# Two copies and a sum of the first layer moved off VectorE: last states to ScalarE, the sum over directions to identity products

## The chip, the cores and the metric

The kernel runs on one core of one Trainium2 chip. The metric is the device time of one execution in microseconds (us): the median of three runs of the kernel before is 18365.06 us, between 18352.45 and 18369.7. A core has five engines with a queue each: TensorE (PE in the profile; its weight loads are PEld), VectorE (DVE), ScalarE (ACT), GpSimd (POOL) and SyncE (SP, which issues DMAs). Each works through its instructions in a fixed order and waits at an instruction until what it needs is there; what stands behind that instruction waits too.

## What is computed

The network has two layers; the change concerns only the mixing part of the first. There, eight images of 64x64 pixels with 128 channels pass through a state-space scan in four directions (rows forward and backward, columns forward and backward), and the four results are weighted and added:

```python
U = jnp.stack([xp, jnp.flip(xp, 1), x_tb, jnp.flip(x_tb, 1)], 0)
Y = jax.vmap(_mamba)(U, ...)
# in _mamba, for each of 128 channels and 16 states:
#   h = exp(dt * A) * h + (dt * x) * B ;  y = sum over states of h * C
#   y = (y + x * D) * silu(z) ;  return y @ out_w.T
y_fused = gate[0] * y_lr + gate[1] * y_rl + gate[2] * y_tb + gate[3] * y_bt
```

The gate, the output weights and the final projection are folded into one 128x128 matrix for each direction, so the kernel only has to add four products into one image-sized result.

## The kernel before

**Tiles.** A direction `d` of an image (4096 pixels) is cut into four chunks `j` of `CH` = 1024 pixels; a chunk has 16 groups of 8 channels with their 16 states, 128 rows in all. A group of a chunk is one slot `n` of the loop in `scan_blocks` (line 703): 8 images x 4 directions x 4 chunks x 16 groups = 2048 slots. Below, slot 0 to 15 count within a chunk.

**One slot.** In slot `n`, TensorE spreads the decays of group `n+1` to its 128 rows by six bf16 products into a PSUM tile `dA` (128x1024, two banks, two such tiles), and ScalarE takes their exponential in place. GpSimd multiplies `bx` for group `n+2`. VectorE then runs the scan of group `n` in place in its `dA` (line 765), multiplies it by `C` into `hc` (line 335), and copies the last column of the scan to `last[:, q]` (a 128x1 copy, line 347), from which the same group of the next chunk starts its scan. The last chunk of a direction (`j` = 3) makes no such copy. A `dA` tile is free for group `n+2` when VectorE has read it.

**A chunk's end.** The output of a chunk gathers in one PSUM tile `y` (two banks), and is finished in the first slots of the next chunk. In slot 1, VectorE multiplies `y` by the gate `zs` (`gate_y`). At the start of slot 2, ahead of the products for the decays of group 3, TensorE multiplies `zs` by the output matrix, half by half, back into `y` (`out_product`; at 17.5 in the table, and halves are rounded up and put at the start of the slot). Then `out_add` brings the two halves of 512 pixels to `r`, the image in SBUF: for `d` = 0 ScalarE copies them, for the other directions VectorE adds them to what stands in `r`. For directions 1 and 3 the result is reversed on the way; for directions 2 and 3 it is also transposed, so that `r` is read and written with 64 elements between neighbours.

**The next chunk.** In slots 1 to 4, ScalarE and VectorE also compute the step sizes of the chunk that starts at the next slot 0, for two halves (0 and 1): ScalarE `relu_abs`, `exp`, `plus_one` (`sp_u`), then VectorE `lost` (line 344, which reads `sp_u`), ScalarE `ln`, and VectorE `dt` (two operations on 512 columns). `plus_one(0)` and the second `relu_abs` stand in slot 2, `exp(1)`, `plus_one(1)`, `lost(0)`, `lost(1)`, `ln(0)` and `dt(0)` in slot 3, `ln(1)` and `dt(1)` in slot 4.

**The next image.** While an image is scanned, `input_steps` normalises the next one in eight pieces, one in each chunk. Of a piece's steps, `powers` (two ScalarE activations) falls in slot 2, `second_log` and `unskipped` (two more) in slot 4, of the eight chunks that follow chunks 5 to 12 of an image's sixteen (counted from 0). These stand ahead of the chunk's own steps on the queue.

**Order.** `ordered` (used by `mm`, `act`, `tt`, `copy` and others) chains every recorded instruction behind the one before it on its engine, so the order on each engine is that of the loop: in a slot first the steps at half slots, then the decays and exponential of group `n+1`, `bx`, the scan, `hc` and `last`, and then the table's steps of the slot.

Of the kernel before, what the change touches and what calls it, by code (L numbers as in the profile page):

```python
# [12 lines left out]
ALU = mybir.AluOpType  # L13
# [9 lines left out]
L = 4096  # L23
S = 512
# [5 lines left out]
CH = 1024  # L30
# [239 lines left out]
def bc(ap, n, axis=None):  # L270

    axis = len(ap.shape) if axis is None else axis
    v = ap.unsqueeze(axis)
    shape = list(v.shape)
    shape[axis] = n
    return v.to_broadcast(shape)


class Net:
# [167 lines left out]
    def scan_steps(self, ch, xp, r, pl, ps):  # L447
# [4 lines left out]
        nc, d, j = self.nc, ch["d"], ch["j"]  # L452
        pool = nc.gpsimd
        back = d % 2 == 1
        lo = L - CH * (j + 1) if back else CH * j
        dtb, cb2 = self.w(f"dt_b{d}"), self.cb2[:, d : d + 1]
        start = [lo + (1 - q if back else q) * S for q in range(2)]
        half = [slice(q * S, (q + 1) * S) for q in range(2)]
        ID, TANH = AF.Identity, AF.Tanh
        v = {}  # L460

        def order(ap):
            return ap[:, ::-1] if back else ap
# [5 lines left out]
        def make(name, bufs, width=S):  # L469
            t = v[name] = pl.tile([C, width], F32, name=name.rstrip("01"), bufs=bufs)  # L470
            return t
# [4 lines left out]
                o = start[q] + (6 - t if back else t)  # L476
                self.mm(p, self.Wt[:, d, t, :], xp[:, o : o + S], start=t == 0, stop=t == 3)

        def gate(name, to, q, **kw):
            p = v[f"{name}{q}"]  # L480
            self.act(order(to[:, half[q]]), p, ID, scale=0.5, **kw)
            th = make(f"th{q}", 2)
            self.act(order(th), p, TANH, scale=0.5, **kw)
            self.act(th, th, ID, bias=self.k("one"))

        def gated(of, name, q):
            to = of[name][:, half[q]]
            self.tt(to, to, v[f"th{q}"], ALU.mult, pool)

        def x_gate(q):  # L490
            if q == 0:
                ch["xs"] = make("xs", 3, CH)
            gate("x", ch["xs"], q, bias=cb2)

        def z_product(q):
            self.mm(bank(f"z{q}"), self.w(f"z_w{d}"), xp[:, start[q] + PAD : start[q] + PAD + S])
# [1 line left out]
        def z_gate(q):  # L498
            if q == 0:
                make("zs", 1, CH)  # L500
            gate("z", v["zs"], q)

        def dt_product(q):
            self.mm(bank(f"d{q}"), self.Wd[:, d, :], ch["xs"][:, half[q]])
# [58 lines left out]
                self.mm(ch["y"][rows_, half[q]], self.D_diag[:, rows_], ch["xs"][:, half[q]], start=False)  # L563

        def gate_y():
            self.tt(v["zs"], ch["y"], v["zs"], ALU.mult)

        def out_product(q):
            self.mm(ch["y"][:, half[q]], self.Wo[:, d, :], v["zs"][:, half[q]])

        def out_add(q):
            p, lo = ch["y"][:, half[q]], CH * j + q * S
            lo = L - S - lo if back else lo
            if d < 2:
                to = r[:, lo : lo + S]
                to = to[:, ::-1] if back else to
            else:
                w0 = lo // 64
                to = r.rearrange("p (h w) -> p w h", w=64)[:, w0 : w0 + S // 64, :]
                to = to[:, ::-1, ::-1] if back else to  # L580
                p = p.rearrange("p (w h) -> p w h", h=64)
            if d == 0:
                self.ordered(nc.scalar.copy(to, p))
            else:
                self.tt(to, to, p, ALU.add)

        table = [
            (-23, taps, 0, (0, 1)), (-22, taps, 0, (2, 3)), (-21, taps, 1, (0,)), (-20, taps, 1, (1,)),
            (-19, taps, 1, (2, 3)), (-21, x_gate, 0), (-18, x_gate, 1), (-20, gated, ch, "xs", 0), (-17, gated, ch, "xs", 1),
            (-16, dt_product, 0), (-15, dt_product, 1), (-16, self.table, EXP_LN_SET),  # L590
            (-15, relu_abs, 0), (-15, exp, 0), (-14, plus_one, 0), (-14, relu_abs, 1), (-13, exp, 1), (-13, plus_one, 1),
# [4 lines left out]
            (-9, self.table, EXP_TANH_SET), (-8, part, 1, 1), (-8, rest, 1, 0), (-7, rest, 1, 1),  # L596
            *([(12, diagonal)] if j == 0 else []),
            (7, z_product, 0), (8, z_product, 1), (8, z_gate, 0), (9, z_gate, 1),
            (10, gated, v, "zs", 0), (11, gated, v, "zs", 1),
            (16, skip, 0), (16, skip, 1), (17, gate_y), (17.5, out_product, 0), (17.5, out_product, 1),  # L600
            (18, out_add, 0), (18, out_add, 1),
        ]
        return table
# [99 lines left out]
    def scan_blocks(self, r, xp, xt, pl, ps):  # L703
# [4 lines left out]
        nc = self.nc  # L708
# [27 lines left out]
        last = None  # L736
        for n in range(min(todo), max(todo) + 1):
            for step, args in ahead.pop(n, ()):
                step(*args)
            u = n + 1  # L740
            if 0 <= u < total:

                ch, q = chunks[u // NQ], 4 * (u % 4) + u % NQ // 4
                dA[u] = ps.tile([128, CH], F32, tag="dA", bufs=2, name="dA")
                sel = self.expand[:, 8 * q : 8 * q + 8, :].rearrange("p c n -> p (c n)")
                for h in range(2):
                    sg = slice(h * S, (h + 1) * S)
                    for i in range(3):
                        self.mm(dA[u][:, sg], sel, ch["parts"][:, i, sg], start=i == 0, stop=i == 2)
                self.act(dA[u], dA[u], AF.Exp, scale=self.negA[:, ch["d"] * NQ + q : ch["d"] * NQ + q + 1])  # L750
            u = n + 2
            if 0 <= u < total:
                bx[u] = pl.tile([128, CH], F32, name="bx", bufs=4)
                self.tt(bx[u], xE.pop(u), chunks[u // NQ]["B16"], ALU.mult, nc.gpsimd)
            u = n + 4
            if 0 <= u < total:
                ch, q = chunks[u // NQ], 4 * (u % 4) + u % NQ // 4
                xE[u] = pl.tile([128, CH], F32, name="xE", bufs=4)
                nc.sync.dma_start(xE[u], bc(ch["dtx"][8 * q : 8 * q + 8, :], NST, 1))
            if 0 <= n < total:  # L760
                ch, q = chunks[n // NQ], 4 * (n % 4) + n % NQ // 4
                if n % NQ == 0 and ch["j"] == 0:
                    last = pl.tile([128, NQ], F32, name="last", bufs=2)
                t = dA.pop(n)
                self.ordered(nc.vector.tensor_tensor_scan(  # L765
                    out=t, data0=t, data1=bx.pop(n), initial=0.0 if ch["j"] == 0 else last[:, q : q + 1],
                    op0=ALU.mult, op1=ALU.add,
                ))
                hcs[n] = pl.tile([128, CH], F32, name="hc", bufs=5)
                self.tt(hcs[n], t, ch["C16"], ALU.mult)  # L770
                if ch["j"] < NCH - 1:
                    self.copy(last[:, q : q + 1], t[:, CH - 1 :], nc.vector)
            if n % 4 == 0 and 4 <= n < total + 4:
                g0 = n - 4
                ch, k = chunks[g0 // NQ], g0 % NQ // 4
                if k == 0:
                    ch["y"] = ps.tile([C, CH], F32, tag="y", bufs=1, name="y")
                for h in range(2):
                    for g in range(4):
                        self.mm(ch["y"][32 * g : 32 * g + 32, h * S : (h + 1) * S],  # L780
                                self.k("collect")[:, 32 * k : 32 * k + 32],
                                hcs[g0 + g][:, h * S : (h + 1) * S], start=k == 0, stop=False)
                for g in range(4):
                    del hcs[g0 + g]
            for step, args in todo.pop(n, ()):
                step(*args)
# [1116 lines left out]
```

## Time and profile before

| what | value |
| --- | --- |
| median of 3 runs | 18365.06 us |
| the profiled execution | 18370.72 us, its span 18368.8 us |
| end of the first layer's scans | the last add to `r` starts at 8525.3 us |
| VectorE busy from 2000 to 4000 us | 1931 of 2000 us |
| TensorE, GpSimd, ScalarE busy there | 1581, 1600, 1214 us |
| scan, 1536 that start from `last` | 2350 ns each |
| `hc` | 1225 ns each |
| copy to `last`, 1536 | 148 ns each |
| add to `r`, 192 | 675 ns least, 1259 ns median |
| copy to `r` by ScalarE (`d` = 0), 64 | 592 ns each |

The profile is one execution recorded by the hardware. A row of a timeline gives the start in us, the duration in us, the engine, the line (often that of a helper), the operation, the tiles written and read, and the count; in square brackets stands how long the engine had been idle before, and what released it. Where an instruction is a matrix product of fp32, TensorE shows two records for one `matmul`.

### The profile page before, as it was taken

The numbers are of one execution on the slowest core, as the hardware profiler recorded it, in microseconds if no ns is written. First come the engines' busy times: TensorE is split into PE (matmuls) and PEld (weight loads), VectorE is DVE, ScalarE is ACT, GpSimd is POOL, SyncE is SP. The second block draws the span as 40 slices with busy tenths as digits, with TensorE's granted clock in tenths as the row PEclk, the third lists the DMA queues.
The fourth block names the chain that finished last, engine by engine and source line by source line (L and its number), as shares of the span: only waits on it lengthen the run. The fifth ranks groups of instructions, "written<-read, shape, count | busy, mean of one in ns | idle before, by whom it ended". The sixth has DMA issues, their size and how long they took to land. (4 is left out here: it accounts for less than half of the span.)

```text
span 18368.8 us, 300240 instructions
## 1 busy us (share of the span) xinstructions
PE 15729.2 (86%) x114341; PEld 8435.2 (46%) x114341; DVE 15174.0 (83%) x20453; ACT 11208.4 (61%) x15902; POOL 9306.3 (51%) x6308
## 2 busy tenths in 40 slices
PE   7777777787777778776887999999999999998998
PEld 2222222222222222223644677777777777774443
DVE  7999999999999999998264677777777777777886
ACT  5656666565666656554253667776777767676553
POOL 7878788787878878774011222222222222222444
PEclk9999999999999999998698999999999999998999
DMA  4555555555455555553442111111111111111222
GB/s 131 143 144 147 145 145 143 143 144 146 143 144 146 142 146 145 143 138 112 140 146 68 28 31 30 30 31 31 31 29 31 31 31 29 31 31 40 93 95 82
DMA packets 843742, 1734.86 MB, mean 94 GB/s; under 512 B 184315, under 2 KB 416667, under 8 KB 833883
## 3 DMA queue, kind: packets, MB, share of 16 engines
q1 hardware_dynamic: 842302, 1715.66, 32.6%
q8 instruction: 904, 14.81, 0.3%
q14 instruction: 536, 4.39, 0.1%
HBM read 1474.28 MB, written 241.04 MB: 93 GB/s over the span
## 5 line engine op out<-in xcount | busy, mean ns | idle before, releaser
L335 POOL TENSOR_TENSOR bx<-xE,B 128x1024 f32<-128x1024 f32 x2048 | 4811.6, 2359 | 320.8 <-DMA xE<-dtx_d 161.8
L288 PE MATMUL dA<-parts,expand 128*128 128x512 bf16 x12288 | 3194.6, 399 | 1719.2 <-DVE last L347 1301.2
L296 ACT ACTIVATE dA<-dA,negA 128x1024 f32<-128x1024 f32 x2048 | 2229.8, 1089 | 2948.9 <-PE dA L288 2942.4
L765 DVE TENSOR_TENSOR_SCAN dA<-dA,last,bx 128x1024 f32<-128x1024 f32 x1536 | 3609.7, 2350 | 91.1 <-ACT dA L296 81.3
L288 PEld LDWEIGHTS <-expand 128*128 128x128 bf16 x12288 | 1128.1, 100 | 4140.1 <-DVE last L347 2110.4
L344 DVE SCALAR_TENSOR_TENSOR E_cm<-E_cm,gm_cm 128x1024 f32<-128x1024 f32 x2048 | 2440.5, 1227 | 280.2 <-ACT E_cm L296 267.6
L335 DVE TENSOR_TENSOR hc<-dA,C 128x1024 f32<-128x1024 f32 x2048 | 2508.2, 1225 | 107.8 <-DVE dA L765 1.8
L1279 POOL COPY Sd_cm<-S_cm 64x128 f32<-64x128 f32 x1024 | 882.7, 862 | 2622.5 <-DVE S_cm L335 2533.1
L296 ACT ACTIVATE E_cm<-ss_p 128x1024 f32<-128x1024 f32 x2048 | 1981.5, 1021 | 266.0 <-PE ss_p L288 253.1
L335 POOL TENSOR_TENSOR xD_cm<-tok_cm,D_cm 128x256 f32<-128x256 f32 x512 | 404.5, 790 | 2374.0 <-PE y_p L288 2306.8
L288 PE MATMUL y_p<-E_cm,pad_cm 128*32 128x128 f32 x32768 | 1321.3, 277 | 119.6 <-DVE E_cm L344 118.6
L765 DVE TENSOR_TENSOR_SCAN dA<-dA,bx 128x1024 f32<-128x1024 f32 x512 | 1172.3, 2290 | 50.5 <-ACT dA L296 42.9
L288 PE MATMUL ss_p<-ssB_cm,ssA_cm 128*128 128x512 bf16 x4096 | 1090.5, 383 | 71.9 <-DVE gm_cm L335 44.2
L288 PE MATMUL y<-hc,kt 128*32 128x512 f32 x8192 | 1087.7, 651 | 3.6 <-DVE hc L335 3.6
L288 PEld LDWEIGHTS y_p<-E_cm,pad_cm 128*32 128x32 f32 x32768 | 903.7, 110 | 369.1 <-DVE E_cm L344 202.5
L288 PE MATMUL bc_p<-stk_cm,W_cm 128*128 128x256 f32 x4096 | 943.2, 384 | 26.4 <-DMA stk_cm<-xs 20.8
L1136 DVE COPY dtr_cm<-tok_p 128x16 f32<-128x16 f32 x1024 | 176.8, 173 | 867.1 <-ACT tok_cm L296 867.1
L288 PEld LDWEIGHTS bc_p<-stk_cm,W_cm 128*128 128x128 f32 x4096 | 770.8, 191 | 167.3 <-issue 28.4
L288 PE MATMUL tok_p<-W_cm,stk_cm 128*128 128x200 f32 x4096 | 749.5, 336 | 0.0
L344 DVE SCALAR_TENSOR_TENSOR dw<-h,w_second,dw 128x512 f32<-128x512 f32 x1024 | 723.1, 748 | 1.5 <-ACT h L296 1.1
L296 ACT ACTIVATE tok_cm<-tok_p 128x384 f32<-128x384 f32 x1024 | 503.1, 491 | 345.5 <-DVE dtr_cm L1136 183.0
L288 PEld LDWEIGHTS tok_p<-W_cm,stk_cm 128*128 128x128 f32 x4096 | 683.1, 190 | 52.2 <-ACT BC_cm L296 48.5
(432 smaller groups left out, 29590.8 us busy)
## 6 DMA issues: line engine op xcount, KB each, us to landing
xE<-dtx_d SPq DMA_DIRECT2D x2048, 512.0 KB
dtx_d<-dtx SPq DMA_DIRECT2D x256, 256.0 KB
x<-x SPq DMA_DIRECT2D x256, 256.0 KB
pb<-p_d SPq DMA_DIRECT2D x64, 1024.0 KB
ssA_cm<-cs_cm SPq DMA_DIRECT2D x3072, 4.0 KB
stk_cm<-xs SPq DMA_DIRECT2D x368, 128.0 KB
stk_cm<-y SPq DMA_DIRECT2D x368, 128.0 KB
px<-r SPq DMA_DIRECT2D x64, 256.0 KB
```

The costliest lines, as they stand in the source:

```text
L288: return self.ordered(self.nc.tensor.matmul(out, lhsT=lhsT, rhs=rhs, start=start, stop=stop))
L296: i = self.ordered(self.nc.scalar.activation(out, in_, func, **kw))
L335: self.ordered((eng or self.nc.vector).tensor_tensor(out, a, b, op))
L344: self.ordered(self.nc.vector.scalar_tensor_tensor(out=out, in0=a, scalar=s, in1=b, op0=op0, op1=op1))
L765: self.ordered(nc.vector.tensor_tensor_scan(out=t, data0=t, data1=bx.pop(n), initial=0.0 if ch["j"] == 0 else last[:, q : q + 1], op0=ALU. ...
L1136: nc.vector.tensor_copy(dtr[:, c, jj, :], v[:, :, cfg.wsil :])
L1279: nc.gpsimd.tensor_copy(Sd[gr, :, g * hi : (g + 1) * hi], S2[gr])
```

## The change

The 1536 copies to `last` become ScalarE copies, at the same place of the loop, which on ScalarE is behind the exponential of group `n+1`. For directions 1 to 3, each half of the output is followed by a product of the identity matrix with the piece of `r` that it is to be added to, accumulated in the same PSUM bank, and ScalarE copies the sum back to `r`, as it did for `d` = 0. So that the sum needs no reversal, `zs` of the backward directions is now written in the image's order, and `gate_y` reads `y` reversed.

```diff
-        def gate(name, to, q, **kw):
+        def gate(name, to, q, order=order, **kw):
             p = v[f"{name}{q}"]
-            self.act(order(to[:, half[q]]), p, ID, scale=0.5, **kw)
+            self.act(order(to), p, ID, scale=0.5, **kw)
...
-            to = of[name][:, half[q]]
+            to = of[name][:, half[1 - q if back and name == "zs" else q]]
...
-            gate("x", ch["xs"], q, bias=cb2)
+            gate("x", ch["xs"][:, half[q]], q, bias=cb2)
...
-            gate("z", v["zs"], q)
+            gate("z", v["zs"][:, half[1 - q if back else q]], q, lambda ap: ap)
...
         def gate_y():
-            self.tt(v["zs"], ch["y"], v["zs"], ALU.mult)
+            self.tt(v["zs"], order(ch["y"]), v["zs"], ALU.mult)
+
+        def rows_of(ap, q):
+            at = lo + q * S
+            if d < 2:
+                return ap[:, at : at + S]
+            return ap.rearrange("p (h w) -> p w h", w=64)[:, at // 64 : (at + S) // 64, :]
+
+        def out_bank(q):
+            p = ch["y"][:, half[q]]
+            return p if d < 2 else p.rearrange("p (w h) -> p w h", h=64)
 
         def out_product(q):
-            self.mm(ch["y"][:, half[q]], self.Wo[:, d, :], v["zs"][:, half[q]])
+            self.mm(ch["y"][:, half[q]], self.Wo[:, d, :], v["zs"][:, half[q]], stop=d == 0)
+            if d:
+                self.mm(out_bank(q), self.k("ident"), rows_of(r, q), start=False)
 
         def out_add(q):
...
-            if d == 0:
-                self.ordered(nc.scalar.copy(to, p))
-            else:
-                self.tt(to, to, p, ALU.add)
+            self.ordered(nc.scalar.copy(rows_of(r, q), out_bank(q)))
...
                 if ch["j"] < NCH - 1:
-                    self.copy(last[:, q : q + 1], t[:, CH - 1 :], nc.vector)
+                    self.ordered(nc.scalar.copy(last[:, q : q + 1], t[:, CH - 1 :]))
```

More of the change, by code (lines that the diff above doesn't have):

```diff
@@ L565, in gate_y @@
         def gate_y():
-            self.tt(v["zs"], ch["y"], v["zs"], ALU.mult)
+            self.tt(v["zs"], order(ch["y"]), v["zs"], ALU.mult)
[7 more added lines that the diff above has]
+            return p if d < 2 else p.rearrange("p (w h) -> p w h", h=64)
         def out_product(q):
-            self.mm(ch["y"][:, half[q]], self.Wo[:, d, :], v["zs"][:, half[q]])
+            self.mm(ch["y"][:, half[q]], self.Wo[:, d, :], v["zs"][:, half[q]], stop=d == 0)
+            if d:
+                self.mm(out_bank(q), self.k("ident"), rows_of(r, q), start=False)
         def out_add(q):
[L572 to L576, printed above, removed]
-            else:
[L578 to L581, printed above, removed]
-            if d == 0:
-                self.ordered(nc.scalar.copy(to, p))
-            else:
-                self.tt(to, to, p, ALU.add)
+            self.ordered(nc.scalar.copy(rows_of(r, q), out_bank(q)))
         table = [
```

## The prediction

> **What bounds the kernel now.** I read first the busy times, for the whole span and for a stretch of the first layer, then VectorE's groups there, then its timeline in undisturbed slots, and last the engines' timelines where a chunk is finished. The first layer's scans end at about 8.5 ms; the rest of the 18.4 ms is not touched.
>
> ```profile
> span 18368.8 us, 300240 instructions
> ...
> core 0: us, PE busy (x) PEld busy (x) DVE busy (x) ACT busy (x) POOL busy (x), PEclk, DMA share, GB/s
> 2000.00:4000.00 2000.00, 1580.91 (x6551) 552.01 (x6552) 1930.98 (x1611) 1213.88 (x1616) 1599.96 (x879) 0.95 0.52 144
> ```
>
> VectorE is busy 97% of the stretch: it is the bound, and whatever it waits for is added to the span. ScalarE has 61%, which looks like room, but an average says nothing of the slots where a chunk is finished.
>
> ```profile
> L347 DVE COPY last<-dA 128x1 f32<-128x1 f32 x1277 | 188.6, 148 | 0.0
> L335 DVE TENSOR_TENSOR r<-r,y x192: 675/1259/1293, 457.9 to 8525.3; 128x512 f32<-128x512 f32 x192
> L583 ACT COPY r<-y x64: 588/592/597, 198.6 to 7742.5; 128x512 f32<-128x512 f32 x64
> ```
>
> The first row is a group's busy time and mean; the other two give shortest/median/longest. An add to `r` takes 675 ns for direction 1 (reversed) and about 1260 ns for 2 and 3 (transposed).
>
> ```profile
> 3722.24 2.36 DVE L765 TENSOR_TENSOR_SCAN dA<-dA,last,bx 128x1024 f32<-128x1024 f32 x1
> 3724.63 1.22 DVE L335 TENSOR_TENSOR hc<-dA,C 128x1024 f32<-128x1024 f32 x1
> 3725.77 0.15 DVE L347 COPY last<-dA 128x1 f32<-128x1 f32 x1
> 3725.84 2.35 DVE L765 TENSOR_TENSOR_SCAN dA<-dA,last,bx 128x1024 f32<-128x1024 f32 x1
> 3728.22 1.22 DVE L335 TENSOR_TENSOR hc<-dA,C 128x1024 f32<-128x1024 f32 x1
> 3729.36 2.35 DVE L765 TENSOR_TENSOR_SCAN dA<-dA,last,bx 128x1024 f32<-128x1024 f32 x1
> ```
>
> Here a chunk with copies passes into one without (`j` = 3). The slot with the copy lasts 3.60 us (3.59 is usual), that without 3.52: a copy is worth 0.067 us, not its 148 ns, since it overlaps its neighbours.
>
> Now the finish of a chunk of direction 0, where ScalarE already copies and VectorE adds nothing (slots 2 and 3):
>
> ```profile
> 3409.17 1.98 PE L288 MATMUL y<-zs,W_out 128*128 128x512 f32 x4 [0.66 <-DVE zs L335]
> 3410.99 1.46 PE L288 MATMUL dA<-parts,expand 128*128 128x512 bf16 x6
> 3412.49 1.09 ACT L296 ACTIVATE dA<-dA,negA 128x1024 f32<-128x1024 f32 x1 [1.94 <-PE dA L288]
> 3413.50 1.07 ACT L583 COPY r<-y 128x512 f32<-128x512 f32 x2
> 3413.68 2.36 DVE L765 TENSOR_TENSOR_SCAN dA<-dA,last,bx 128x1024 f32<-128x1024 f32 x1 [0.97 <-ACT dA L296]
> ...
> 3418.53 0.70 DVE L344 SCALAR_TENSOR_TENSOR m<-sp_u,m 128x512 f32<-128x512 f32 x1 [0.57 <-ACT sp_u L296]
> ...
> 3420.47 2.35 DVE L765 TENSOR_TENSOR_SCAN dA<-dA,last,bx 128x1024 f32<-128x1024 f32 x1
> ```
>
> and of direction 2, where VectorE adds:
>
> ```profile
> 3931.32 1.98 PE L288 MATMUL y<-zs,W_out 128*128 128x512 f32 x4
> 3933.14 1.46 PE L288 MATMUL dA<-parts,expand 128*128 128x512 bf16 x6
> ...
> 3935.16 2.45 DVE L335 TENSOR_TENSOR r<-r,y 128x512 f32<-128x512 f32 x2
> ...
> 3937.50 2.35 DVE L765 TENSOR_TENSOR_SCAN dA<-dA,last,bx 128x1024 f32<-128x1024 f32 x1
> ...
> 3943.82 2.35 DVE L765 TENSOR_TENSOR_SCAN dA<-dA,last,bx 128x1024 f32<-128x1024 f32 x1
> ```
>
> In direction 0 the time without adds is not won: scan 3 waits 0.97 us for its exponential, which stands behind the output products on TensorE, and `lost(1)` waits 0.57 us for ScalarE, which made the copies first. In direction 2 the adds fill exactly this hole. From scan 2 to scan 4 (scan starts in VectorE's timeline, averaged over the six middle images) it takes 10.9 us after direction 0, 11.1 after 1, 12.2 after 2 and 3.
>
> **The change, part by part.** Removed copies to `last`: 12 of a chunk's 16 slots end on VectorE's own work (scans 2, 3 and 4 and slot 1 end on the waits above), so 12 x 0.067 = 0.8 us in each of 96 chunks: **-77 us**. The new ScalarE copy has no row of its shape; the nearest, an activation of 128x8 out of PSUM, takes 177 ns, so I take 0.2 us (ends 0.1 and 0.3). In a plain slot it is hidden: it stands behind the exponential for group n+1, which ends some 0.85 us before scan n+1 wants it (a plain one in the same trace ends at 3925.54, and its scan starts at 3926.39). Without that cover it would cost 0.2 us a slot. It is not hidden in slots 2 and 3, below.
>
> Sum over directions, TensorE. Two more fp32 products are four more records, which start 0.455 us apart in the rows above ((3933.14 - 3931.32) / 4): +1.82 us ahead of the products for decay 3, and nothing else stands there. Exponential 3 is late by as much; behind it on ScalarE wait the copy to `last`, the `powers`, the two copies to `r` and the step sizes; VectorE waits at scan 3 and then at `lost(1)`.
>
> The price of a boundary follows from direction 0. From the end of `gate_y` (about 3409.03) to scan 4 (3420.47) it takes 11.44 us. The new boundary is that plus 1.82 plus two small copies in the chain, 0.4: 13.66 us, and `powers` add 1.2 (the two activations take 0.66 + 0.53 us of ScalarE there). Before, from the same point, it is about 11.5 after direction 1 and 12.65 after 2 and 3 (the averages above and some 0.4 us of wait for exponential 2). So each boundary loses: direction 1 2.15, with `powers` 3.35; directions 2 and 3 1.0, with `powers` 2.2. That is with the adds' 1.2 and 2.4 us already taken off.
>
> `powers` are there after chunks 5 to 12: three of direction 1, four of 2, one of 3. An image: 2.15 + 3 x 3.35 + 4 x 2.2 + 2.2 + 3 x 1.0 = 26.2; the last image has none: 4 x 2.15 + 8 x 1.0 = 16.6. 7 x 26.2 + 16.6 = 200, less 24 chunks without copies to `last` x 0.4: **+190 us**. Direction 0 gets the two small copies alone, 24 x 0.4: **+10 us**.
>
> Slot 4. There the small copy waits for scan 4, which starts only after `dt(0)`; ScalarE used to be past that. Behind it stand `second_log` and `unskipped` (0.61 us each) and `ln(1)` (0.62), for which VectorE waits at `dt(1)`: ready 0.3 + 1.2 + 0.6 + 0.1 = 2.2 us after scan 4, when `hc` leaves VectorE free after 1.25. 0.9 us in 6 of the 8 such chunks of seven images, 42 x 0.9: **+38 us**. In slot 6 the copies of the input steps come 0.2 us later and hold a TensorE product that already waits for them: 42 x 0.2, **+8 us**. Where no input step is there, `ln(1)` is ready after 1.0 us and hidden by `hc`.
>
> The transposed `r` (directions 2 and 3, 64 boundaries). No row has TensorE read, or ScalarE write, with 64 elements between neighbours. The nearest is the same tile in VectorE's add: 1259 against 675 ns, 1.14 ns an element more, but there both sides are strided. [...] By the row's extra, the two copies cost 2 x 0.58 and the four records 4 x 0.58 = 2.3 us; by nothing, 0. [...] For ScalarE I take a doubling of the streamed part, 2 x 512 x 0.83 ns = 0.85 us (0.83 from 1021 ns for 1024 and 597 for 512 columns in its exponentials); for TensorE, where no row is near, about half of a doubling, 0.9. Both lie in the chain: 64 x 1.75 = **+112 us**, ends 0 and 64 x 3.5 = 225.
>
> `zs` written unreversed costs nothing (all 256 writes take 588 to 592 ns, reversed or not). `gate_y` reading reversed: the reversed add took 675 ns where a plain operation of that size takes 686, so nothing; at the doubling of the transposed row it would be 64 x 1.2 = 77.
>
> **Sum**: -77 + 190 + 10 + 38 + 8 + 112 = +281 us, on a span of 18368.8 within 18370.7; on the median of 18365, **18645 us**.
>
> **Rivals.** (1) Transposed access is free: 18645 - 112 = 18534. For it: no row of these engines shows a price. (2) It costs as much on each as on VectorE: 18645 + 113 = 18758. Both are ends of the same forecast. (3) VectorE stays the bound and what it loses in work is won: 64 boundaries x 2.35 + 32 x 1.2 + 77 = 266 us, **18100**. Its place is slot 2; it holds if output products, decay products and exponential 3 end before `hc` of group 2. They need 1.82 + 1.82 + 1.5 + 1.1 = 6.2 us after `gate_y` and have 3.6 to 3.9; it decides from 2.4 us less. VectorE's 97% speak for it, direction 0 against it. (4) The small copies hold up ScalarE in every slot, since each waits for the scan: 1536 x 0.2 on top, about 18950. Against it stands the 0.85 us of room. (5) The new waits are made good in later slots by what the removed work frees, and it ends level, 18365; but the plain slots before show VectorE without a wait that could shrink.
>
> **Numbers.** The forecast with its two ends 0.74 (own range 18534 to 18758), (3) 0.09, (4) 0.11, (5) 0.06. A change under 0.2% (37 us) can't be told from none: faster 0.09, same 0.05, slower 0.86. For 8 in 10 the range reaches a little beyond the ends: 18470 to 18790.
>
> **What would show it.** In the profile after: no VectorE row for `last` or `r`; VectorE idle before scan 3 for exponential 3 (2 to 4 us) and before `lost(1)` for `sp_u`, after directions 1 to 3; plain slots of 3.52 us; idle before `dt(1)` in chunks with input steps; TensorE's identity records and ScalarE's `r` copies longer for directions 2 and 3 if the strides cost. It is wrong if scan 3 starts on time, if plain slots are not shorter, or if the small copies take much over 0.3 us.

## The result

The changed kernel takes 18820.63 us (median of 4 runs, 18809.22 to 18830.5) where the kernel before takes 18360.6: a ratio of 1.0249, 95% interval 1.0237 to 1.0262. It is 460 us slower. Forecast were 281 us more, 18645, in a range of 18470 to 18790: the direction was right, the size was not, and the time lies 31 us beyond the range. (18360.6 is a median of four runs; the 18365 that the forecast started from is one of three.)

### The profile page after: what moved, and what is told of

It is laid out like the page before. It is cut to its first block, busy times and chain, and to the rows that moved or that the text cites. A ratio compares the mean times of both kernels' runs of the same rounds, so it can differ in the third digit from the quotient of the medians.

```text
span 18807.4 us, 299313 instructions
## 1 busy us (share of the span) xinstructions
PE 15986.3 (85%) x113668; PEld 8605.5 (46%) x114725; DVE 14884.6 (79%) x18725; ACT 11483.7 (61%) x17630; POOL 9304.5 (49%) x6308
## 5 line engine op out<-in xcount | busy, mean ns | idle before, releaser
L288 PEld LDWEIGHTS <-expand 128*128 128x128 bf16 x12288 | 1217.5, 101 | 4198.4 <-issue 2631.2
L288 PE MATMUL ss_p<-ssB_cm,ssA_cm 128*128 128x512 bf16 x3582 | 1039.5, 382 | 109.8 <-DVE gm_cm L335 44.7
L771 ACT COPY last<-dA 128x1 f32<-128x1 f32 x1536 | 248.9, 162 | 1088.8 <-DVE hc L335 1078.3
L335 POOL TENSOR_TENSOR dtx<-sp_r,xs 128x512 f32<-128x512 f32 x256 | 324.5, 1268 | 842.7 <-DVE sp_r L335 832.2
```

What stands on the lines that cost most here:

```text
L288: return self.ordered(self.nc.tensor.matmul(out, lhsT=lhsT, rhs=rhs, start=start, stop=stop))
L335: self.ordered((eng or self.nc.vector).tensor_tensor(out, a, b, op))
L771: self.ordered(nc.scalar.copy(last[:, q : q + 1], t[:, CH - 1 :]))
```

## The profile after

The same views as before, of the changed kernel: its span, and the busy times of the stretch from 2000 to 4000 us.

```profile
span 18807.4 us, 299313 instructions
...
2000.00:4000.00 2000.00, 1564.30 (x6216) 562.17 (x6330) 1775.83 (x1142) 1220.46 (x1926) 1525.91 (x839) 0.95 0.50 137
```

VectorE (third engine of the row) is busy 1776 us where it was busy 1931. The work did leave it; it now waits instead, and the first layer takes longer. The timeline of VectorE in two plain slots, both with a copy to `last` that is now ScalarE's:

```profile
4123.97 2.35 DVE L764 TENSOR_TENSOR_SCAN dA<-dA,last,bx 128x1024 f32<-128x1024 f32 x1
4126.35 1.23 DVE L335 TENSOR_TENSOR hc<-dA,C 128x1024 f32<-128x1024 f32 x1
4127.49 2.35 DVE L764 TENSOR_TENSOR_SCAN dA<-dA,last,bx 128x1024 f32<-128x1024 f32 x1
```

3.52 us from scan to scan, as forecast. Now the finish of the same chunk of direction 2 that was shown of before (chunk `j` = 1 of the fourth image), from the timelines of TensorE, ScalarE and VectorE, slots 2 and 3:

```profile
4132.36 1.11 PE L288 MATMUL y<-zs,W_out 128*128 128x512 f32 x2
4133.32 1.88 PE L288 MATMUL y<-r,kt 128*128 128x512 f32 x2
...
4135.89 1.87 PE L288 MATMUL y<-r,kt 128*128 128x512 f32 x2
4137.59 1.48 PE L288 MATMUL dA<-parts,expand 128*128 128x512 bf16 x6
...
4139.10 1.09 ACT L296 ACTIVATE dA<-dA,negA 128x1024 f32<-128x1024 f32 x1 [3.81 <-PE dA L288]
4140.11 0.16 ACT L771 COPY last<-dA 128x1 f32<-128x1 f32 x1
4140.15 0.64 ACT L296 ACTIVATE q<-psq 128x512 f32<-128x512 f32 x1
...
4141.36 1.90 ACT L584 COPY r<-y 128x512 f32<-128x512 f32 x2
...
4140.29 2.36 DVE L764 TENSOR_TENSOR_SCAN dA<-dA,last,bx 128x1024 f32<-128x1024 f32 x1 [3.72 <-ACT last L771]
4147.20 0.70 DVE L344 SCALAR_TENSOR_TENSOR m<-sp_u,m 128x512 f32<-128x512 f32 x1 [2.69 <-ACT sp_u L296]
4149.13 2.35 DVE L764 TENSOR_TENSOR_SCAN dA<-dA,last,bx 128x1024 f32<-128x1024 f32 x1
```

The two waits that the forecast named are there: 3.72 us before scan 3 and 2.69 before `lost(1)`. (The first is put down to `last`, but scan 3 starts 0.1 us after the end of the exponential.) The adds of 2.45 us are gone, and slots 2 and 3 take 16.2 us, from the scan at 4132.96 to 4149.13, where they took 12.3. One slot further on, in ScalarE's and VectorE's timelines, stands what the forecast had not seen:

```profile
4149.13 2.35 DVE L764 TENSOR_TENSOR_SCAN dA<-dA,last,bx 128x1024 f32<-128x1024 f32 x1
4151.51 1.23 DVE L335 TENSOR_TENSOR hc<-dA,C 128x1024 f32<-128x1024 f32 x1
...
4152.77 0.16 ACT L771 COPY last<-dA 128x1 f32<-128x1 f32 x1 [2.92 <-DVE hc L335]
...
4154.06 0.62 ACT L296 ACTIVATE sp_u<-sp_u 128x512 f32<-128x512 f32 x1
...
4154.71 0.70 DVE L335 TENSOR_TENSOR m<-sp_u,m 128x512 f32<-128x512 f32 x1 [1.98 <-ACT sp_u L296]
```

The scan whose last column is copied ends at 4151.48. The copy does not start then but at 4152.77, when `hc` has ended. Behind it on ScalarE wait two activations of the next image and `ln(1)` (at 4154.06), and for `ln(1)` VectorE stands idle 1.98 us. In the kernel before, the same `ln(1)` and the `dt(1)` that needs it, in the slot that starts with the scan at 3943.82:

```profile
3946.26 0.62 ACT L296 ACTIVATE sp_u<-sp_u 128x512 f32<-128x512 f32 x1
3947.41 0.69 DVE L335 TENSOR_TENSOR m<-sp_u,m 128x512 f32<-128x512 f32 x1
```

There `ln(1)` started 2.4 us after the scan, here 4.9, and VectorE did not wait. The same hold comes back in slot 6, where ScalarE copies the next image's input (`pxc`) behind the copy to `last`. From the timelines of ScalarE, TensorE and VectorE in a chunk of the sixth image, whose slot 6 starts at 6375.01:

```profile
6378.65 0.16 ACT L771 COPY last<-dA 128x1 f32<-128x1 f32 x1 [0.67 <-DVE hc L335]
6378.70 0.59 ACT L630 COPY pxc<-m 128x512 f32<-128x512 f32 x1
...
6379.85 1.12 PE L288 MATMUL m<-xs,W_bc 128*128 128x512 f32 x2 [1.86 <-ACT psq L296]
...
6383.56 2.36 DVE L764 TENSOR_TENSOR_SCAN dA<-dA,last,bx 128x1024 f32<-128x1024 f32 x1 [1.42 <-ACT last L771]
```

The copy of `pxc` starts 3.7 us after the slot does, where it started after 2.7 in the kernel before. A TensorE product waits for what follows it, the products for the decays of group 8 stand behind that one, and VectorE waits 1.42 us before scan 8. (Again this is put down to `last`, but the scan starts 0.1 us after the end of exponential 8.)

For the whole layer I took the starts of all 2048 scans from both timelines and summed, over the 128 chunks, how much longer each slot became:

| slots | us longer, all chunks | forecast |
| --- | --- | --- |
| 1 (wait for exponential 2) | 23 | 0 |
| 2 and 3 (boundary) | 283 | 190 + 10 + 112 |
| 4 (`ln(1)`) | 126 | 38 |
| 6 and 7 | 84 | 8 |
| 12 (`D_diag` in `j` = 0) | -48 | 0 |
| 0, 5, 8 to 11, 13 to 15 | -22 | -77 (with some of the slots above) |
| sum | 447 | 281 |

The first scan starts 1.4 us earlier and what follows the last is 6.7 us shorter, which makes the 438.6 us between the two spans.

## The experiments

Each run is compared with the kernel before on the same chip. "Slots" are again sums of differences of scan starts.

**The sum alone.** The copies to `last` go back to VectorE; the rest of the change stays.

```diff
-                    self.ordered(nc.scalar.copy(last[:, q : q + 1], t[:, CH - 1 :]))
+                    self.copy(last[:, q : q + 1], t[:, CH - 1 :], nc.vector)
```

> The change with the copies to last back on VectorE; only the sum over directions is made by identity products and copied by ScalarE. Theory A (the copy to last waits for hc, because ScalarE may read a dA tile only after VectorE has read it, and so holds up ScalarE in slots 4 and 6): the losses of slots 4, 6 and 7 go, those of slots 2 and 3 stay, about +280 us on the kernel before: 18640. Rival B (the surplus over the forecast comes from the identity products and the copies to r): it stays near the changed kernel, 18790.

Measured: 18665.64 us, ratio 1.0165 (1.015 to 1.018), about 302 us more than before. Slots 2 and 3 lose 294 us, slots 4, 6 and 7 nothing (0.6, 0.0, -0.2). The boundary loss belongs to the sum, and the rest of the 460 to the copies.

**The copies alone.** The kernel before, with only the copies to `last` on ScalarE.

```diff
-                    self.copy(last[:, q : q + 1], t[:, CH - 1 :], nc.vector)
+                    self.ordered(nc.scalar.copy(last[:, q : q + 1], t[:, CH - 1 :]))
```

> The kernel before with only the copies to last on ScalarE; the sum stays on VectorE. Theory A: slots 4, 6 and 7 lose what they lost in the changed kernel (126 + 17 + 67 us), plain slots gain about 40 to 80: 18480 to 18530. As the prediction had it (the copy waits for the scan alone): -77 + 38 + 8, 18320. Rival B: no loss, about 18290.

Measured: 18581.0, ratio 1.012 (1.0103 to 1.0137), 217 us more; more than any of the three had it. Slot 4 loses 127 us, slots 6 and 7 90, slot 3 49, slot 1 23; slot 12 wins 45, the plain ones 0.06 each. In the changed kernel slot 3's 49 us are hidden behind the boundary's longer wait, so the two halves (302 + 217) add up to more than the whole. The tile `last` in this kernel, with the rows of what ended ScalarE's or VectorE's idle time before its instructions (us, times):

```profile
L772 ACT COPY last<-dA x1536: 159/159/173, 125.6 to 8668.3; 128x1 f32<-128x1 f32 x192
...
  DVE hc L335: 1221.3, 1051
```

1051 of the 1536 copies wait for `hc`, 1.16 us each; none is said to wait for a scan. Here and in the changed kernel, none of the 1536 starts before its slot's `hc` has ended.

**A constant in place of the last column.** ScalarE's copy reads SBUF instead of `dA`.

```diff
-                    self.ordered(nc.scalar.copy(last[:, q : q + 1], t[:, CH - 1 :]))
+                    self.ordered(nc.scalar.copy(last[:, q : q + 1], self.negA[:, q : q + 1]))
```

> As e2, but ScalarE fills last from a constant in SBUF instead of the scan's last column, so it waits for nothing that VectorE does (the scans start from wrong states: that part of the computation is left out). Theory A: the time of the copies is free and their wait is all: slots 4 and 7 as before, plain slots 0.07 us shorter, 18270. Rival C (the copy itself, 0.16 us on ScalarE's queue, is what costs): near e2.

Measured: 18377.85, ratio 1.0007 (0.9997 to 1.0016): level. My expectation was wrong in that the copy "waits for nothing that VectorE does": it overwrites the column that the scan of this slot starts from, so it waits for the scan.

```profile
L772 ACT COPY last<-negA x1536: 175/181/235, 122.8 to 8473.8; 128x1 f32<-128x1 f32 x192
...
  DVE dA L765: 195.1, 165
```

So this is the copy as the prediction had taken it, waiting for the scan alone, in the chunks `j` = 1 and 2: none of their 1024 copies starts before its scan has ended. In the first chunk of a direction (`j` = 0) no scan reads `last`, and 103 of the 512 copies start before their scan has ended. Slot 4 loses 0.5 us in chunks with input steps, which is 0.8 for `j` = 1 and 2 (forecast 0.9) and nothing for `j` = 0; it wins 0.06 in the others. Slot 7 loses 0.44 with input steps, plain slots win 0.06, and slot 12 loses 24 us. 165 copies wait, where 1051 did. The step from here to waiting for `hc` is 18581 - 18378 = 203 us. It is the price of two things together, the hold on ScalarE's queue and that on the `dA` tile, since the copy of a constant does not read the tile; the rows of slots 4 and 6 above show the first at work.

**Waiting for nothing.** As above, with a fresh tile for each chunk's states.

```diff
-                if n % NQ == 0 and ch["j"] == 0:
-                    last = pl.tile([128, NQ], F32, name="last", bufs=2)
+                if n % NQ == 0:
+                    was, last = last, pl.tile([128, NQ], F32, name="last", bufs=3)
...
-                    out=t, data0=t, data1=bx.pop(n), initial=0.0 if ch["j"] == 0 else last[:, q : q + 1],
+                    out=t, data0=t, data1=bx.pop(n), initial=0.0 if ch["j"] == 0 else was[:, q : q + 1],
```

> As e3, but each chunk writes a fresh tile for its last states, so that ScalarE's copy from the constant does not even wait for the scan that reads the old one (the states are wrong as in e3). Theory A (waits are all, the copy itself is free): the remaining losses of e3 in slots 4 and 7 (0.5 and 0.44 us in chunks with input steps) go too, about 40 us less than e3: 18330. Rival C (0.16 us on ScalarE's queue costs): as e3, 18378.

Measured: 18328.32, ratio 0.9981 (0.9971 to 0.999). Slot 4's loss is gone in all chunks (-0.06 each). Here a copy of 0.18 us on ScalarE costs nothing by itself; its waits are the price. The gain of some 32 us is less than the 77 that the plain slots seemed to promise; in the profiled run, the slowest of ten, slots 1 and 12 took 20 and 12 us back.

**The copy ahead of `hc`.** Only the order of recording is turned round in the kernel with the copies alone.

```diff
-                hcs[n] = pl.tile([128, CH], F32, name="hc", bufs=5)
-                self.tt(hcs[n], t, ch["C16"], ALU.mult)
                 if ch["j"] < NCH - 1:
                     self.ordered(nc.scalar.copy(last[:, q : q + 1], t[:, CH - 1 :]))
+                hcs[n] = pl.tile([128, CH], F32, name="hc", bufs=5)
+                self.tt(hcs[n], t, ch["C16"], ALU.mult)
```

> As e2 (only the copies to last on ScalarE), with the copy recorded ahead of hc, so that it reads dA first. If the two engines' reads of a dA tile are kept apart in the order recorded, hc now waits for the copy, which stands behind the exponential for group n+1: about 0.5 us in each of 1536 slots, 19100; and ScalarE's losses in slots 4 and 7 shrink. If hc and the copy were free to overlap, as the prediction took it: near e3, 18380.

Measured: 19440.35, ratio 1.0589 (1.0573 to 1.0605), 1080 us more. Now `hc` is what waits; of the tile `hc`:

```profile
  ACT last L770: 1399.7, 1536
```

All 1536 wait, 0.91 us each. Both instructions only read `dA`, and neither order let them overlap: the second reader waited for the first, whichever was recorded first (1.16 us in each of 1051 copies with `hc` first, 0.91 us in each of 1536 `hc` with the copy first). The expectation of 19100 was low because in slots 1 and 2, where exponentials 2 and 3 are late anyway, the copy behind them holds `hc` too (1.7 and 3.2 to 3.7 us in chunks with copies, 0.4 in a plain slot).

**The copy behind the slot's steps.** In the kernel with the copies alone, so that no step waits for the copy.

```diff
             for step, args in todo.pop(n, ()):
                 step(*args)
+            if 0 <= n < total and chunks[n // NQ]["j"] < NCH - 1:
+                self.ordered(nc.scalar.copy(last[:, q_n : q_n + 1], t_n[:, CH - 1 :]))
```

(`t_n` and `q_n` are the slot's scan tile and group; the copy at the old place goes.)

> As e2 (only the copies to last on ScalarE), with the copy behind all of the slot's steps on ScalarE's queue, so that none of them waits for it. If the held steps were the whole of e2's loss, this is at or below the kernel before: about 18300. Theory A goes further: the copy also holds the dA tile, so the products for group n+2 and the exponential behind them now wait for the slot's steps; slots 4 and 7 recover, and slots with over 1.5 us of steps (3, 6, 8, 9, 11, 14) lose 0.3 to 1 us each: about 18550.

Measured: 19504.51, ratio 1.0617 (1.0603 to 1.0632), 1139 us more. The direction is theory A's: the `dA` tile now comes free behind the steps. The size is not; I had overlooked that this closes a ring, in which each part waits for the one before it. From the merged timeline (all engines) in slots with gate steps:

```profile
3000.53 1.46 PE L288 MATMUL dA<-parts,expand 128*128 128x512 bf16 x6 [2.38 <-ACT last L787]
...
3002.09 1.09 ACT L296 ACTIVATE dA<-dA,negA 128x1024 f32<-128x1024 f32 x1 [1.60 <-PE dA L288]
...
3005.34 0.15 ACT L787 COPY last<-dA 128x1 f32<-128x1 f32 x1
...
3005.54 1.46 PE L288 MATMUL dA<-parts,expand 128*128 128x512 bf16 x6 [0.64 <-ACT last L787]
```

Products, exponential, steps, copy, and then the next products: 5.0 us for this slot in place of 3.6. In chunks with copies, slots 7, 8, 9 and 15 take 5.0 to 5.4 us on average, and slot 3 loses 2.4; slots 6, 11 and 14, which I had named, lose next to nothing. TensorE's mean granted clock is 0.931 here and 0.954 in the kernel before; how much of the loss comes of that was not separated.

**What in the sum costs: the transposed access.** The sum alone, with `r` read and written in plain order for all directions.

```diff
-            if d < 2:
-                return ap[:, at : at + S]
-            return ap.rearrange("p (h w) -> p w h", w=64)[:, at // 64 : (at + S) // 64, :]
+            return ap[:, at : at + S]
...
-            return p if d < 2 else p.rearrange("p (w h) -> p w h", h=64)
+            return p
```

> As e1, but the identity products and the copies of directions 2 and 3 read and write r without transposing (the sums land in wrong places; otherwise the same work). If the step of 64 elements costs, as the longer records of the changed kernel say (identity records 1.02 instead of 0.59 us, copies up to 1.1 instead of 0.6): 64 boundaries x (4 x 0.43 + 2 x 0.5) = 174 us less than e1, 18470. If it is hidden: as e1, 18640.

Measured: 18512.49, ratio 1.0083 (1.0068 to 1.0098), 153 us less than the sum alone. The tile `r` in both, shortest/median/longest in ns; first the sum alone, then this one:

```profile
L288 PE MATMUL y<-r,kt x384: 592/1017/1038, 453.6 to 8816.9; 128*128 128x512 f32 x192
L584 ACT COPY r<-y x256: 567/802/1095, 197.1 to 8818.8; 128x512 f32<-128x512 f32 x128
```

```profile
L288 PE MATMUL y<-r,kt x384: 592/592/593, 451.1 to 8674.2; 128*128 128x512 f32 x192
L582 ACT COPY r<-y x256: 567/589/601, 196.6 to 8675.3; 128x512 f32<-128x512 f32 x128
```

**What in the sum costs: the identity products.** The sum alone without them; the copies stay.

```diff
-            if d:
-                self.mm(out_bank(q), self.k("ident"), rows_of(r, q), start=False)
```

> As e1, but without the identity products: the copies to r stay, and the sum over directions is left out. If TensorE's four records ahead of the products for decay 3 set the loss at a boundary, 1.83 us of the loss go after direction 1 and 3.5 after 2 and 3 (records of 1.02 us): 32 x 1.83 + 64 x 3.5 = 283 less than e1, 18385. If ScalarE's copies set it (0.5 to 0.95 us each ahead of sp_u), most of the loss stays: above 18550.

Measured: 18391.0, ratio 1.0016 (1.0007 to 1.0025), 275 us less than the sum alone. A boundary wins back 1.69 us after direction 1, 3.39 after 2 and 3.38 after 3: the four records, plain and strided, almost to the full. What is left, ScalarE's copies, slightly outweighs the adds that VectorE no longer makes: 27 us over all boundaries.

**The same work in another order.** The sum alone, with the products behind those for the decays, the copies at the end of slot 3, and `exp(1)` and `plus_one(1)` before exponential 4.

```diff
-            (-14, relu_abs, 1), (-13, exp, 1), (-13, plus_one, 1),
+            (-14, relu_abs, 1), (-14, exp, 1), (-14, plus_one, 1),
...
-            (17.5, out_product, 0), (17.5, out_product, 1),
-            (18, out_add, 0), (18, out_add, 1),
+            (18, out_product, 0), (19, out_product, 1),
+            (19.5, out_add, 0), (19.5, out_add, 1),
```

> As e1 (copies to last on VectorE), with the same work in another order: the output and identity products of half 0 in slot 2 and of half 1 in slot 3 behind the products for the decays, the two copies to r at the end of slot 3, and exp(1) and plus_one(1) in slot 2. If the losses of slots 2 and 3 are a matter of what stands in front of the exponential and of sp_u, as the boundary sum says, scans 3 and 4 wait for nothing, slots 2 and 3 take 9.8 us after every direction, where the kernel before has 10.9, 11.1, 12.2, 12.2: about 230 us less than before, 18135. If TensorE or ScalarE have no room for the added work there: above 18360.

Measured: 18211.91, ratio 0.9918 (0.9901 to 0.9934), 149 us less than before. The same boundary of direction 2, VectorE's timeline:

```profile
3873.56 2.36 DVE L764 TENSOR_TENSOR_SCAN dA<-dA,last,bx 128x1024 f32<-128x1024 f32 x1 [0.29 <-ACT dA L296]
...
3877.16 2.35 DVE L764 TENSOR_TENSOR_SCAN dA<-dA,last,bx 128x1024 f32<-128x1024 f32 x1
...
3883.97 2.35 DVE L764 TENSOR_TENSOR_SCAN dA<-dA,last,bx 128x1024 f32<-128x1024 f32 x1
```

Scan 3 follows without a wait, and slots 2 and 3 take 10.4 us (12.3 before, 16.2 in the changed kernel); with the same identity products, still strided. They win 191 us in all: 1.0 us after direction 0, where VectorE had no adds to lose and the order alone can have won it, and 0.9, 1.9 and 2.3 after 1, 2 and 3. Slot 1 gave 39 back, waiting longer for exponential 2, and in chunks with input steps `ln(0)` still comes 0.5 us late.

**And the skip products earlier.** The same, with `skip` made in slots 14 and 15 of its own chunk (the last group's products then close the sum in PSUM).

```diff
-            (16, skip, 0), (16, skip, 1), (17, gate_y), ...
+            (14, skip, 0), (15, skip, 1), (17, gate_y), ...
```

> As e7, and the products of D with x (skip) are made in slots 14 and 15 of the chunk, not in slot 0 of the next one, where they stand on TensorE ahead of the products for decay 2. If e7's remaining wait before scan 2 (0.9 us a chunk on average, 0.3 us where TensorE's clock is full) comes of that queue, most of it goes: about 75 us less than e7, 18135. If it comes of something else there (GpSimd, the y products): as e7, 18210.

Measured: 18027.26 (five rounds), ratio 0.9817 (0.9804 to 0.983), 338 us less than the kernel before and 185 less than the last: more than twice what I expected. Slot 1 alone wins 129 us on it: VectorE's wait before scan 2, 0.93 us a chunk, is gone altogether. The mean granted clock of TensorE is 0.972 where the kernel before has 0.954, and fewer of the decay products are slow: a slot's six take 1.47 us in the median, and over 1.9 in 165 slots before, in 73 with the last order and in 21 here. How much of the gain comes of that was not separated. This is the fastest of all.

## Why the prediction was wrong

**The failed step** is slot 4: "There the small copy waits for scan 4". It waits for `hc` of slot 4, 1.25 us later. I took two instructions that only read `dA` to be free to overlap; the prediction does not say so, but its sums for slots 4 and 6 rest on it. The two reads of the tile were kept apart in the order recorded, as the row of waits in the copies-alone run (1051 copies, 1.16 us each for `hc`) and the reversed order (1536 `hc`, 0.91 us each for the copy) both show. From there the surplus follows. `ln(1)` holds VectorE in every chunk with copies, not only in those with input steps (0.8 us without, 2.0 with; forecast 0 and 0.9), so slot 4 costs 126 us for 38. ScalarE's input copies in slot 6 start about 1.2 us late, not 0.2, and hold a TensorE product for slot 7, so slots 6 and 7 cost 84 for 8. That is 164 us over the forecast, where the whole table is 166 over it: the errors of the other terms, which follow, come to almost nothing together, and that is luck. With the constant, where two thirds of the copies wait for the scan and none for `hc`, slots 4, 6 and 7 together cost 30 us, near the 46 forecast. None of the three signs that the prediction named for being wrong came; that the copy might wait for something else was not among them.

**Removed copies**: 0.067 us a plain slot was right (3.52 from scan to scan). The 77 us did not come in full, since slots such as 6, 9, 13 and 14 began to wait. (Of the four slots that the sum sets apart, it names one twice: slot 1 ends with scan 2.)

**Four more records ahead of the decays**: right. 1.82 us forecast, 1.69 measured after direction 1.

**The transposed `r`**: mis-sized. The forecast took 112 us, with a doubling of the streamed part for ScalarE and half of one for TensorE. Both were my estimates, and no row of before shows either; the runs of the sum show nearly a full doubling on both engines: two strided identity records take 1.88 us and two copies 1.90 where plain ones take 1.02 and 1.07, and 153 us went when the stride went; with a full doubling on both engines the forecast would have been 64 x (1.7 + 0.85) = 163. TensorE's share is the larger: without the identity products a boundary of directions 2 and 3 won back 1.7 us more than one of direction 1, of the 2.4 us that it won without the stride.

**Two small copies in the boundary's chain**: 0.4 us forecast, about 0.1 true. The activation behind the copy starts 0.04 us after it (4140.11 and 4140.15). Direction 0 lost nothing (-0.05 us a boundary for 0.3), direction 1 2.2 instead of 2.9. The sum alone, which has no such copies, loses 2.2 there as well, so some 0.3 us of direction 1's surplus lies elsewhere and stays open. These overestimates and the stride's underestimate partly cancelled, again by luck: the boundary measured 283 us for 312.

**Reversal**: right. `gate_y` takes 1214 ns reading reversed and took 1215 before.

**Not in the sum at all**: slot 12 won 48 us (the last section says of what) and slot 1 lost 23.

**The rivals**: the removed work was not won (3), as direction 0 had said. Rival (4), that the small copies hold up ScalarE, had the right place but the wrong reason and size: a hold in all 1536 slots for 300 us more. It was a hold that VectorE felt in a few slots of a chunk, and most plain slots have room for it. (5), that later slots make it good, did not come: slots 5, 8, 10 and 11 win the copy's 0.06 us and no more.

## What to carry to other kernels

When work moves to another engine, ask what else reads the same PSUM tile: a read by a second engine may have to wait for the first one's (here 1.16 us in 1051 of 1536 copies), and everything behind it on its in-order queue waits as well (`ln(1)` started 4.9 us after its slot's scan instead of 2.4). An engine with 40% idle time (ScalarE was busy 1214 of 2000 us) can still be the last to arrive in the few slots where a chunk ends (scan 3 waited 3.72 us); price a move there, slot by slot, with a boundary that already works that way as the model. The sum over directions lost 1.6% ahead of the exponential and, in another order with the skip products moved out of the way, was part of a kernel 1.8% faster than before. No run has that order with the adds still on VectorE, so what the sum itself adds to the 1.8% is not shown.

## What the runs showed of the hardware that was not expected

`D_diag`, a VectorE operation on 128x128, took 1549 ns in the median before and 350 after, with nothing about it changed. In the kernel before, 23 of the 32 start while GpSimd multiplies a `bx`, and most of these end with it:

```profile
3056.63 4.67 POOL L335 TENSOR_TENSOR bx<-xE,B 128x1024 f32<-128x1024 f32 x2
...
3056.99 2.07 DVE L339 TENSOR_SCALAR D_diag<-kt,w_first 128x128 f32<-128x128 f32 x1
```

The first of the two multiplications ends near 3059.0, and `D_diag` at 3059.06. In the changed kernel the slots before are late, and it meets the end of a shorter GpSimd operation instead (`xs` in 24 cases and `r` in 8, 1.27 us each, where a `bx` takes 2.35): together the 32 take 13 us, where they took 55, which is most of the 48 us that slot 12 won. All the traces agree: of the 384 `D_diag` in the twelve kernels, 382 end 0.06 to 0.11 us after the end of a GpSimd operation, while at most 4% of the `hc` of any kernel do. So in all but two cases `D_diag` ended just after a GpSimd operation, whichever that was; that GpSimd blocks it is inferred from this, since no run took GpSimd's operation away.
